# Third head's softmax before a slot's first piece, MLP layer norms on ScalarE within the fc products, weight sums in halves, the last product by token tiles

## Chip, cores and metric

One core of a Trainium2 chip. The metric is the device time of one execution in microseconds (us), the median of several runs. The engines run side by side and wait for one another by semaphores: PE (TensorE, matmuls and transposes), DVE (VectorE), ACT (ScalarE), POOL (GpSimd) and SP (SyncE, which here only issues DMA transfers). Each engine works off its own instructions in their given order, so an instruction that waits holds up all behind it on that engine.

## The reference

A block of cross attention with an MLP behind it, in float32, for 8 batches of 256 tokens, width D = 512, 16 heads of 32, inner width 2048:

```python
def layer_norm(x, w, b):
    mu = jnp.mean(x, axis=-1, keepdims=True)
    var = jnp.mean(jnp.square(x - mu), axis=-1, keepdims=True)
    return (x - mu) * jax.lax.rsqrt(var + EPS) * w + b
...
residual = hidden_states
x = layer_norm(hidden_states, ln1_w, ln1_b)
q = (x @ q_w + q_b)       # k and v the same from encoder_hidden_states; split into 16 heads
scores = jnp.einsum('bhqd,bhkd->bhqk', q, k) * scale
scores = jnp.where(mask, scores, mask_value)
attn = jax.nn.softmax(scores, axis=-1)
out = jnp.einsum('bhqk,bhkd->bhqd', attn, v)
out = out @ cproj_w + cproj_b
hidden = out + residual
residual = hidden
y = layer_norm(hidden, ln2_w, ln2_b)
y = jax.nn.gelu(y @ fc_w + fc_b, approximate=True)
y = y @ proj_w + proj_b
return residual + y
```

## The kernel before

**Tiling.** The tokens go in four groups g of 512 (two batches each). All large products (q, k, v, the output projection, fc and proj) are Strassen products in Winograd's form: the two operands are cut in quarters "11", "12", "21", "22", sums of quarters ("s1" to "s4" of one side, "t1" to "t4" of the other) are made by DVE or POOL, and PE does seven products of quarters in place of eight. A product's result is in a PSUM bank; DVE adds banks and stored sums (u1, u2, u3) into the four quarters of the result. u1 is a copy by ACT, u2 = bank 6 + u1, u3 = bank 7 + u2; the quarters of fc's result are called h, and x within group 0.

**Attention, 0 to 343 us.** Lines 866 to 897 write out the order by hand. There are 32 units, one for each group of four heads and batch. Unit n issues the scores of unit n+2 (PE, `s`, L572), then the softmax of unit n+2's four heads one by one between other work. `softmax(n, j)` is, twice, a masked row maximum on DVE (L590) and an exp on ACT (L600). `turn_probs(n, j)` transposes a head's probabilities (PE, `ppt`, L625), which DVE copies to `pt` for head 0 and ACT for heads 1 to 3 (L630). `divide(n+1)` is four multiplications on POOL (L614). `attend(n)` multiplies pt with v (PE, `av`, L641). Between these stand, in two slots of each unit (`between[g, u, 0]` and `[g, u, 1]`), pieces of other groups' Strassen products: a few matmuls (L367) and their evacuation on DVE or ACT (L386, L384). The unit's order before is: scores and softmax 0 of n+2; transposes 0 and 1; divide; softmax 1; the first slot's pieces; softmax 2; transposes 2 and 3; softmax 3; the second slot's pieces; attend. The transposes and av share two PSUM buffers.

**Output projection, 343 to 355 us.** Group 3's `po`.

**MLP, from 355 us.** For each group: fc with gelu, then proj with the residual added (`resm`, in the code `ht`), and the result stored.

- Group 0's fc (355.1 to 404.4 us) goes by quarter-columns q = 0 to 3. In each of them PE does the seven products in the order 11·11, s2·t2, s3·12, 21·t1, 12·21, 22·t4, s4·22. In the last two quarter-columns `splits` forms further sums of fc's weights (`split_sums`, four operations of 128x256 for each quarter n and half r), which the groups 1 to 3 use. They are formed in a `stage` of three buffers used in turn (`w_stage` in the trace), and two DMAs on SP store each set to `w2_dram` (L973, L974); a buffer is free when its stores have landed. The table `SPLITS` says which engine forms which set at which of the places 0 to 2 of a quarter-column.
- Groups 1 to 3's fc is seven `product(k)` calls with weights read back from `w2_dram`.
- The proj part is seven products `py` between which stands the next group's layer norm: statistics on DVE (L194, L195), roots on POOL (L199, L200) and the normalisation of four token tiles on DVE (`hm`, L203), all issued after the first and second product. `turn_next(c)` then transposes a column chunk of hm (PE, `pyt`, L216) and DVE scales it into y (L244). The loads of hm (`load_hid`, SP, L179) are issued by `load_next`: in group 0 after quarter-column 0, in the others after product 1.
- The last product of a group is 22·t4 on a bank that already holds a product; its sum is added to `ht` (L927) and two token tiles of 128x512 are stored (L1281).

`add` (L927) is a helper: operations of DVE and POOL in the MLP all carry its line, and are told apart by their tiles.

Of the kernel before, what the change touches and what calls it, by code (L numbers as in the profile page):

```python
# [16 lines left out]
P = 128  # L17
# [5 lines left out]
def tile_xattn_block(  # L23
# [100 lines left out]
    def col(base, i):  # L124
        return cols[:, base + i : base + i + 1]
# [60 lines left out]
    def layer_norm(tiles, tag, eng=nc.vector):  # L186


        mv = small.tile([P, NT, 2], F32, tag="mv", name=f"mv_{tag}")
        rstd = small.tile([P, NT], F32, tag="rstd", name=f"rstd_{tag}")  # L190

        def stats(t):
            st = small.tile([P, nc.vector.BN_STATS_DIM], F32, tag="st", name=f"st_{tag}_{t}")
            nc.vector.bn_stats(st, tiles[t])  # L194
            nc.vector.bn_aggr(mv[:, t, :], st)  # L195

        def roots():
            ve = small.tile([P, NT], F32, tag="ve", name=f"ve_{tag}")
            nc.gpsimd.tensor_scalar_add(ve, mv[:, :, 1], EPS)  # L199
            nc.gpsimd.tensor_tensor(rstd, ve, neg_half, ALU.pow)  # L200

        def normalise(t):
            eng.tensor_scalar(  # L203
                tiles[t], tiles[t], mv[:, t, 0:1], rstd[:, t : t + 1], ALU.subtract, ALU.mult
            )
# [34 lines left out]
    def turn_hid(ps, g, c):  # L240
        if c == 0:
            ys[g] = tokens_operand(both, "cT", f"y_{g}")
        turn(ps, hids[g], c)
        nc.vector.tensor_scalar(  # L244
            chunk(ys[g], c), halves(ps), col(c_ln2w, c), col(c_ln2b, c), ALU.mult, ALU.add
        )


    with ExitStack() as att:
# [557 lines left out]
        def run(pieces):  # L807
            for p in pieces:
                p()
# [57 lines left out]
        for n, (g, hg, b) in enumerate(units):  # L867
            u = hg * GB + b
            ahead = n + 2 < len(units)
            if ahead:  # L870
                scores(n + 2)
                softmax(n + 2, 0)
            run(aside[g, u, 0])
            turn_probs(n, 0)
            turn_probs(n, 1)
            if n + 1 < len(units):
                divide(n + 1)
            if ahead:
                softmax(n + 2, 1)
            run(between[g, u, 0])  # L880
            if ahead:
                softmax(n + 2, 2)
            turn_probs(n, 2)
            turn_probs(n, 3)
            run(aside[g, u, 1])
            if ahead:
                softmax(n + 2, 3)
            run(between[g, u, 1])
            run(aside[g, u, 2])
            attend(n)  # L890
            run(later)
            later.clear()
            run(aside[g, u, 3])
# [12 lines left out]
    with ExitStack() as mlp:  # L906
# [19 lines left out]
        def add(eng, to, a, b, op=ALU.add):  # L926
            eng.tensor_tensor(to, a, b, op)  # L927
# [33 lines left out]
        stages = [0]  # L961

        def split_sums(eng, n, r):
            a, b = fcw[r][n], fcw[r + NQF // 2][n]
            st = stage[:, stages[0] % 3]
            stages[0] += 1
            s1, s2, s3, s4 = (st[:, i, :] for i in range(4))
            add(eng, s3, a[:, 0, :], b[:, 0, :], ALU.subtract)
            add(eng, s2, b[:, 1, :], s3, ALU.subtract)
            add(eng, s1, s2, a[:, 0, :])  # L970
            add(eng, s4, a[:, 1, :], s2, ALU.subtract)
            to = w2_dram[QI[n]][:, :, r * S : (r + 1) * S]
            nc.sync.dma_start(to[:, 2, :], s1)  # L973
            nc.sync.dma_start(to[:, 4:7, :], st[:, 1:, :])  # L974

        def keep_quarters(q):

# [43 lines left out]
        for g in range(NG):  # L1021
# [29 lines left out]
            def load_next():  # L1051
                if g + 1 < NG:
                    load_hid(g + 1)

            def bias_ht():

                for b, bias in ((0, projb[:, :HD2]), (1, pbd)):
                    o = out_quarter(b, 0)
                    add(GP, o, o, by_tiles(bias))

            if g == 0:
                y = ys[g]

                def fc(bank, w, b, q, first, last):
# [8 lines left out]
                            )  # L1073

                SPLITS = {
                    (2, 0): ((GP, "11", 0), (V, "12", 0)),
                    (2, 1): ((GP, "s2", 0),),
                    (2, 2): ((V, "s3", 0), (GP, "21", 0)),
                    (3, 0): ((GP, "s4", 0), (V, "22", 0)),
                    (3, 1): ((GP, "11", 1),),  # L1080
                    (3, 2): ((V, "12", 1), (GP, "s2", 1)),
                }

                def splits(q, at):
# [3 lines left out]
                for q in range(NQF):  # L1088
# [4 lines left out]
                    def by_h(t):  # L1093
                        return t.rearrange("p i (d s) -> p d i s", d=2)
# [39 lines left out]
                    gelu("22", 1, x["22"])  # L1134
                    fc(bank[7], "22", "t4", q, False, True)
                    add(V, x["12"], by_h(bank[7]), by_h(u2))
                    some_fc_sums(4)
                    some_pw(2)
                    gelu("12", 1, x["12"])
                    fc(bank[5], "s4", "22", q, False, True)  # L1140
                    add(V, x["21"], by_h(bank[5]), by_h(u2))
                    gelu("21", 0, x["21"])
                    sum_h("s3", q)
                    sum_h("s2", q)
# [6 lines left out]
                        keep_quarters(0)  # L1151
                    if q == 3:
                        bias_ht()
            else:
                gelus, parts = [], [0]

                def some_gelus(n=3):
                    for f in gelus[:n]:
                        f()
                    del gelus[:n]  # L1160
# [17 lines left out]
                def product(k, *sums):  # L1178
# [24 lines left out]

                    def made(cd, n, x):
                        some_gelus()
                        if sums[0][1] is None:
                            add(V, block(sums[0][0], cd), bank[n], x)
                            return

                        r = h["s3"][:, parts[0] % 4 // 2, parts[0] % 2 * HF // 2 :][:, : HF // 2]  # L1210
                        parts[0] += 1
                        add(V, r, bank[n], x)
                        for to, base in sums:
                            add(GP, block(to, cd), block(base, cd), r)
# [29 lines left out]


                product(0, ("21", None))
                product(1, ("11", "21"))
                gelu("11", 0)
                ht = residual(work, hid_dram[g], "resm", f"resm_{g}")
                load_next()  # L1250
                product(2, ("21", "21"))
                product(3, ("12", "21"))
                product(4, ("22", "12"), ("21", "21"))
                product(5, ("21", "21"))
                gelu("21", 0)
                gelu("22", 1)
                product(6, ("12", "12"))
                some_gelus(len(gelus))
                gelu("12", 1)
                for which in ("s3", "s2"):  # L1260
# [3 lines left out]

            bank = {n: bank_of(n, f"py{n}") for n in (1, 7, 6, 5)}

            def proj(bank, a, w, first, last):
                for i in range(2):
# [9 lines left out]
            def store(b):  # L1278
                for i in range(2):
                    r = g * NT + 2 * b + i  # L1280
                    nc.sync.dma_start(of[ts(r, P), :], ht[:, 2 * b + i, :])  # L1281

            def turn_next(c):
                if g + 1 < NG:
# [14 lines left out]
                load_w2(1, 1)  # L1299
            else:  # L1300
                some_gelus(HF)
            if g + 1 < NG:
                seen, roots, normalise = layer_norm(hids[g + 1], f"m{g + 1}")
                for f in (*seen, roots):
                    f()
            for q in range(NQF):
                sum_h("s1", q)
            proj(bank[7], "s3", "12", True, False)
            if g + 1 < NG:
                for f in normalise:  # L1310
                    f()
            if g == 0:
                split_sums(GP, "s4", 1)
                split_sums(V, "22", 1)
# [78 lines left out]
```

## Time and profile before

| what | value |
|---|---|
| median of 3 runs | 745.24 us (745.17 to 746.19) |
| the profiled execution's time | 745.05 us |
| its span in the profile | 743.0 us |
| attention | 0 to 343.0 us |
| group 0: fc, then proj | 355.1 to 404.4, then to 456.4 us |
| groups 1 to 3 | 456.4 to 743.0 us |
| TensorE clock granted | 1.00 throughout |

Busy time by stage, in us, with the counts of instructions; the columns are the stretch, its length, then PE, PE's weight loads, DVE, ACT and POOL, and last the granted clock, the share of the DMA engines and GB/s:

```profile
0.00:343.00 343.00, 339.56 (x2542) 269.23 (x2543) 215.60 (x771) 226.95 (x706) 242.35 (x238) 1.00 0.45 144
343.00:355.10 12.10, 12.10 (x57) 10.65 (x58) 7.74 (x14) 0.47 (x1) 5.31 (x4) 1.00 0.39 116
355.10:404.40 49.30, 48.57 (x225) 42.46 (x224) 28.01 (x38) 15.47 (x33) 41.83 (x41) 1.00 0.86 287
404.40:456.40 52.00, 50.54 (x241) 44.23 (x240) 43.25 (x54) 1.81 (x4) 32.34 (x30) 1.00 0.68 238
456.40:743.00 286.60, 280.48 (x1881) 262.10 (x1879) 139.74 (x199) 53.02 (x120) 159.93 (x130) 1.00 0.38 141
```

PE is busy nearly everywhere, but matmuls are pipelined and their ends are modelled, so a group of matmuls with a wait inside shows as a longer group. The distance from one group's start to the next tells more than the busy share. Idle time of DVE, ACT or POOL costs nothing as long as what they make is there when PE asks for it. Where the profile gives a releaser for a wait, it is inferred.

### The profile page before, as it was taken

How to read it: one execution, taken by the hardware profiler on the slowest of the kernel's cores; microseconds unless marked ns; L12 is line 12 of the kernel's file. 1: busy time of each engine (PE TensorE's matmuls, PEld its weight loads, DVE VectorE, ACT ScalarE, POOL GpSimd, SP SyncE). 2: the span in 40 equal slices, each digit the busy share in tenths (PEclk: the TensorE clock that was granted, in tenths of full speed). 3: DMA queues.
4: the chain of work that ended last, by engine and by line, in shares of the span. 5: the costliest groups of instructions: out<-in, count | busy, mean ns of one | idle time of the engine just before them, and what ended most of it. 6: DMA issues, size and time to landing. Idle time of an engine off the chain costs nothing.

```text
span 743.0 us, 13604 instructions
## 1 busy us (share of the span) xinstructions
PE 731.2 (98%) x4941; PEld 628.7 (85%) x4941; DVE 434.3 (58%) x1075; ACT 297.7 (40%) x864; POOL 481.8 (65%) x441
## 2 busy tenths in 40 slices
PE   9999999999999999999999999999999999999997
PEld 8888777888787777678888789998899988999886
DVE  4676755676456566766267895663456634566111
ACT  2176777765777777761332000232002240031500
POOL 3856679667564469896877970579504796048960
PEclk9999999999999999999999999999999999999999
DMA  9614522552234166532796972992018930172001
GB/s 306 236 58 136 167 83 81 183 171 86 86 100 161 58 209 229 187 109 91 245 348 223 307 280 67 344 361 92 1 57 314 379 116 1 57 270 85 1 1 56
DMA packets 79426, 117.82 MB, mean 159 GB/s; under 512 B 6612, under 2 KB 57856, under 8 KB 77696
## 3 DMA queue, kind: packets, MB, share of 16 engines
q1 hardware_dynamic: 79104, 116.94, 46.0%
q8 instruction: 39, 0.64, 0.4%
q14 instruction: 27, 0.22, 0.1%
q0 software_dynamic: 256, 0.02, 0.0%
HBM read 85.48 MB, written 31.46 MB: 157 GB/s over the span
## 4 chain that ended last, share of the span: by engine, by line
PE 86%; DVE 5%; issue 3%; POOL 3%; ACT 2%; DVEq 0%; POOLq 0%
PE pf L924 23%; PE py L924 19%; PE ppt L625 7%; PE pqT L367 7%; PE pv L367 5%; PE po L367 5%; PE s L572 5%; PE av L641 5%; PE pkT L367 5%; DVE hm L203 2%; PE pkT L464 2%; ACT pr L600 2%; POOL h L927 1%; DVE w_stage L927 1%; PE pxt L216 1%
## 5 line engine op out<-in xcount | busy, mean ns | idle before, releaser
L614 POOL TENSOR_TENSOR pr<-pr,rsum 128x512 f32<-128x512 f32 x128 | 130.2, 1048 | 74.9 <-DVE rsum L612 43.7
L927 POOL TENSOR_TENSOR h<-h,hs 128x512 f32<-128x512 f32 x79 | 98.6, 1276 | 108.8 <-DVE hs L927 108.5
L600 ACT ACTIVATE pr<-pr,nmax 128x256 f32<-128x256 f32 x256 | 128.1, 503 | 61.3 <-DVE nmax L590 61.2
L924 PEld LDWEIGHTS pf<-y,w 128*128 128x128 f32 x1176 | 131.8, 192 | 0.2
L924 PE MATMUL pf<-y,w 128*128 128x128 f32 x1176 | 131.8, 275 | 0.0
L590 DVE CUSTOM_DVE_ANT_0 pr<-s,mb 128x256 f32<-128x256 f32 x256 | 94.0, 413 | 42.0 <-PE s L572 35.0
L1218 ACT COPY u<-pf 128x512 f32<-128x512 f32 x21 | 12.3, 585 | 216.0 <-PE pf L924 216.0
L924 PE MATMUL py<-pw,h 128*128 128x256 f32 x384 | 84.9, 379 | 0.0
L924 PE MATMUL py<-pw_t,h 128*128 128x256 f32 x384 | 84.2, 379 | 0.0
L924 PEld LDWEIGHTS py<-pw_t,h 128*128 128x128 f32 x384 | 72.7, 190 | 9.8
L924 PEld LDWEIGHTS py<-pw,h 128*128 128x128 f32 x384 | 72.5, 190 | 9.6
L625 PEld LDWEIGHTS ppt<-ident,pr 128*128 128x128 f32 x512 | 57.3, 141 | 14.8 <-issue 9.9
L625 PE MATMUL ppt<-ident,pr 128*128 128x128 f32 x512 | 68.7, 276 | 0.2
L927 DVE TENSOR_TENSOR u<-pf,u 128x512 f32<-128x512 f32 x50 | 34.5, 691 | 37.9 <-PE pf L924 33.7
L630 ACT COPY pt<-ppt 128x512 f32<-128x512 f32 x96 | 51.6, 570 | 4.9 <-PE ppt L625 4.9
L367 PE MATMUL pv<-vw,ctxT 128*128 128x256 f32 x224 | 52.4, 380 | 0.0
L367 PE MATMUL pqT<-xnT,qw 128*128 128x256 f32 x224 | 51.2, 380 | 0.3 <-issue 0.3
L924 PE MATMUL pf<-y,fcw 128*128 128x256 f32 x224 | 48.8, 379 | 0.7 <-DVE u L927 0.7
L600 ACT ACTIVATION_READ_ACCUMULATOR pr<-pr,nmax 128x1 f32 x256 | 48.5, 189 | 0.0
L924 PEld LDWEIGHTS pf<-y,fcw 128*128 128x128 f32 x224 | 42.5, 190 | 6.9 <-DVE u L927 1.1
L367 PEld LDWEIGHTS pqT<-xnT,qw 128*128 128x128 f32 x224 | 41.3, 190 | 5.6 <-POOL ctxT L171 0.7
L367 PEld LDWEIGHTS pv<-vw,ctxT 128*128 128x128 f32 x224 | 41.0, 190 | 5.4 <-ACT xnT L341 0.3
(139 smaller groups left out, 1128.0 us busy)
## 6 DMA issues: line engine op xcount, KB each, us to landing
w<-w_dram SPq DMA_DIRECT2D x12, 1792.0 KB, 7.5
w<-in_L_xattn_fc_w_dram SPq DMA_DIRECT2D x27, 256.0 KB, 5.8
w<-w_dram SPq DMA_DIRECT2D x9, 768.0 KB, 7.3
w_dram<-w_stage SPq DMA_DIRECT2D x14, 384.0 KB, 2.9
ctx<-in_ctx_dram SPq DMA_DIRECT2D x16, 256.0 KB, 4.7
x<-in_x_dram SPq DMA_DIRECT2D x16, 256.0 KB, 4.8
v_dram<-st_v SPq DMA_DIRECT2D x16, 256.0 KB, 2.2
v<-v_dram SPq DMA_DIRECT2D x16, 256.0 KB, 3.5
```

Source lines behind the costliest of these rows:

```text
L203: eng.tensor_scalar(tiles[t], tiles[t], mv[:, t, 0:1], rstd[:, t : t + 1], ALU.subtract, ALU.mult)
L367: nc.tensor.matmul(bank[n][:, i, :], l[:, c, ts(i, P)], r[:, c, :], start=first and i == 0 and c == 0, stop=last and c == HC - 1, skip_gro ...
L464: nc.tensor.matmul(bank[:, i, :], w[f"{n[0]}{j + 1}"][:, c, ts(i, P)], x()[f"{j + 1}{n[1]}"][:, c, :], start=at == 0, stop=j == 1 and c == ...
L572: nc.tensor.matmul(banks[j][:, i, :], qT[j * HD : (j + 1) * HD, b * S + i * P : b * S + (i + 1) * P], kT[j * HD : (j + 1) * HD, b * SK : ( ...
L590: nc.vector.tensor_tensor_reduce(pr[:, j, i, :], banks[j][:, i, :], mbias[g][1][:, b, :], scale=-SCALE, scalar=FLT_MAX, op0=ALU.add, op1=A ...
L600: nc.scalar.activation(pr[:, j, i, :], pr[:, j, i, :], AF.Exp, bias=nmax[:, j, i : i + 1], scale=-1.0, accum_out=sums[:, j, i : i + 1],)
L614: nc.gpsimd.tensor_tensor(pr[:, j], pr[:, j], rsum[:, j, :, None].to_broadcast([P, NQ, SK]), ALU.mult,)
L625: nc.tensor.transpose(ps[:, kc, ts(i, P)], probs[n][:, j, i, ts(kc, P)], ident)
L630: nc.scalar.copy(pt, ps)
L641: nc.tensor.matmul(av[j * HD : (j + 1) * HD, :], vs[g, hg][:, b * NK + kc, ts(j, HD)], pts[n, j][:, kc, :], start=(kc == 0), stop=(kc == N ...
L924: nc.tensor.matmul(ps, lhsT, rhs, start=first, stop=last, skip_group_check=True)
L927: eng.tensor_tensor(to, a, b, op)
```

## The change

Four parts.

1. **Attention.** The softmax of the third head (index 2) of unit n+2 is issued ahead of the first slot's pieces instead of behind them.
2. **Layer norm of the next group in the MLP.** `norm_piece` issues one of its small steps at a time: four statistics (DVE), the roots (POOL), and a new `shift` (DVE, −mean·rstd, 128x4). In group 0 they are issued in quarter-columns 1 to 3 after the add of x["12"] and after that of x["21"]; in groups 1 and 2 within products 3 and 4, and after products 5 and 6. The normalisation itself, `normalise_next`, is four ACT instructions (identity with scale rstd and bias shift) instead of four on DVE, issued at the end of group 0's fc, or after the first product of proj in the others. `turn_next` comes two products earlier, and the scaling into y is on ACT for groups 1 to 3. The loads of hm are issued one product earlier in groups 1 and 2.
3. **Group 0's weight sums.** `split_sums` can do its first two or its last two operations; VectorE's sets are issued in two halves at successive places (a new place 3 is behind the add of x["12"]). The two stores of a set are issued with the second half. POOL's sets stay whole.
4. **Last product of the last group.** The right half of the columns of the second pair of token tiles is stored ahead of the last product; the product is issued one token tile after the other, each with its own add of 128x256 and its own store of half a row block.

```diff
@@ attention, one unit
             if ahead:
                 softmax(n + 2, 1)
+                softmax(n + 2, 2)
             run(between[g, u, 0])
-            if ahead:
-                softmax(n + 2, 2)
             turn_probs(n, 2)
@@ turn_hid
-        nc.vector.tensor_scalar(
-            chunk(ys[g], c), halves(ps), col(c_ln2w, c), col(c_ln2b, c), ALU.mult, ALU.add
-        )
+        w, b = col(c_ln2w, c), col(c_ln2b, c)
+        if g == 0:
+            nc.vector.tensor_scalar(chunk(ys[g], c), halves(ps), w, b, ALU.mult, ALU.add)
+        else:
+            nc.scalar.activation(chunk(ys[g], c), halves(ps), AF.Identity, bias=b, scale=w)
@@ split_sums
-        def split_sums(eng, n, r):
+        def split_sums(eng, n, r, half=None):
             a, b = fcw[r][n], fcw[r + NQF // 2][n]
-            st = stage[:, stages[0] % 3]
-            stages[0] += 1
+            if half != 1:
+                staged_sums[n, r] = stage[:, stages[0] % 3]
+                stages[0] += 1
+            st = staged_sums[n, r]
             s1, s2, s3, s4 = (st[:, i, :] for i in range(4))
...
+            if half != 1:
+                add(eng, s3, a[:, 0, :], b[:, 0, :], ALU.subtract)
+                add(eng, s2, b[:, 1, :], s3, ALU.subtract)
+            if half != 0:
+                add(eng, s1, s2, a[:, 0, :])
+                add(eng, s4, a[:, 1, :], s2, ALU.subtract)
+                to = w2_dram[QI[n]][:, :, r * S : (r + 1) * S]
+                nc.sync.dma_start(to[:, 2, :], s1)
+                nc.sync.dma_start(to[:, 4:7, :], st[:, 1:, :])
@@ the layer norm in steps (new)
+            def norm_next():
+                seen, roots, _ = layer_norm(hids[g + 1], f"m{g + 1}")
+                mv, rstd = layer_norm.last
+                nm = small.tile([P, NT], F32, tag="nm", name=f"nm_{g + 1}")
+                def shift():
+                    nc.vector.scalar_tensor_tensor(nm, mv[:, :, 0], -1.0, rstd, ALU.mult, ALU.mult)
+                norm.extend([*seen, roots, shift])
+                return nm, rstd
...
+            def normalise_next():
+                if g + 1 < NG:
+                    nm, rstd = norm_of[0]
+                    for t, xt in enumerate(hids[g + 1]):
+                        nc.scalar.activation(
+                            xt, xt, AF.Identity, bias=nm[:, t : t + 1], scale=rstd[:, t : t + 1]
+                        )
@@ SPLITS
-                    (2, 0): ((GP, "11", 0), (V, "12", 0)),
-                    (2, 1): ((GP, "s2", 0),),
-                    (2, 2): ((V, "s3", 0), (GP, "21", 0)),
-                    (3, 0): ((GP, "s4", 0), (V, "22", 0)),
-                    (3, 1): ((GP, "11", 1),),
-                    (3, 2): ((V, "12", 1), (GP, "s2", 1)),
+                    (2, 0): ((GP, "11", 0), (V, "12", 0, 0)),
+                    (2, 1): ((GP, "s2", 0), (V, "12", 0, 1)),
+                    (2, 2): ((V, "s3", 0, 0), (GP, "21", 0)),
+                    (2, 3): ((V, "s3", 0, 1),),
+                    (3, 0): ((GP, "s4", 0), (V, "22", 0, 0)),
+                    (3, 1): ((GP, "11", 1), (V, "22", 0, 1)),
+                    (3, 2): ((V, "12", 1, 0), (GP, "s2", 1)),
+                    (3, 3): ((V, "12", 1, 1),),
@@ a quarter-column of group 0's fc
                     add(V, x["12"], by_h(bank[7]), by_h(u2))
+                    splits(q, 3)
+                    some_norm(q, 0, 1, 1, 0)
...
                     add(V, x["21"], by_h(bank[5]), by_h(u2))
+                    some_norm(q, 0, 1, 2, 1)
...
                     if q == 3:
                         bias_ht()
+                        normalise_next()
@@ product(k) of groups 1 to 3
                         some_gelus()
+                        if k in (3, 4) and cd != "22":
+                            norm_piece()
...
                 product(0, ("21", None))
+                load_next()
                 product(1, ("11", "21"))
...
-                load_next()
...
                 product(5, ("21", "21"))
+                norm_piece()
...
                 product(6, ("12", "12"))
+                norm_piece()
@@ proj
             else:
                 some_gelus(HF)
-            if g + 1 < NG:
-                seen, roots, normalise = layer_norm(hids[g + 1], f"m{g + 1}")
-                for f in (*seen, roots):
-                    f()
+                normalise_next()
...
             proj(bank[7], "s3", "12", True, False)
-            if g + 1 < NG:
-                for f in normalise:
-                    f()
+            turn_next(0)
+            turn_next(1)
...
-            turn_next(0)
-            turn_next(1)
+            turn_next(2)
+            turn_next(3)
...
-            turn_next(2)
-            turn_next(3)
@@ the last product
-            proj(bank[7], "22", "t4", False, True)
-            o_add(V, 1, 0, bank[7])
-            store(1)
+                proj(bank[7], "22", "t4", False, True)
+                o_add(V, 1, 0, bank[7])
+                store(1)
+            else:
+                store(1, slice(HD2, D))
+                for i in range(2):
+                    proj(bank[7], "22", "t4", False, True, (i,))
+                    o = ht[:, 2 + i, :HD2]
+                    add(V, o, bank[7][:, i, :], o)
+                    store(1, slice(HD2), (i,))
```

More of the change, by code (lines that the diff above doesn't have):

```diff
@@ L190, in layer_norm @@
         rstd = small.tile([P, NT], F32, tag="rstd", name=f"rstd_{tag}")
+        layer_norm.last = mv, rstd
         def stats(t):
@@ L960, in tile_xattn_block @@
         )
-        stages = [0]
-        def split_sums(eng, n, r):
+        stages, staged_sums = [0], {}
+        def split_sums(eng, n, r, half=None):
             a, b = fcw[r][n], fcw[r + NQF // 2][n]
-            st = stage[:, stages[0] % 3]
-            stages[0] += 1
+            if half != 1:
+                staged_sums[n, r] = stage[:, stages[0] % 3]
+                stages[0] += 1
+            st = staged_sums[n, r]
             s1, s2, s3, s4 = (st[:, i, :] for i in range(4))
[L968 to L974, printed above, removed]
+            if half != 1:
[7 more added lines that the diff above has]
+                nc.sync.dma_start(to[:, 4:7, :], st[:, 1:, :])
         def keep_quarters(q):
@@ L1053, in load_next, with norm_piece, some_norm @@
                     load_hid(g + 1)
+            norm = []
+            def norm_next():
[6 more added lines that the diff above has]
+                return nm, rstd
+            def norm_piece():
+                if g + 1 < NG:
+                    if not norm_of:
+                        norm_of.append(norm_next())
+                    norm.pop(0)()
+            norm_of = []
+            def some_norm(q, *ns):
+                for _ in range(ns[q]):
+                    norm_piece()
+            def normalise_next():
+                if g + 1 < NG:
+                    nm, rstd = norm_of[0]
[3 more added lines that the diff above has]
+                        )
             def bias_ht():
@@ L1257, in tile_xattn_block @@
                 product(6, ("12", "12"))
+                norm_piece()
                 some_gelus(len(gelus))
@@ L1265, in tile_xattn_block, with proj @@
             bank = {n: bank_of(n, f"py{n}") for n in (1, 7, 6, 5)}
-            def proj(bank, a, w, first, last):
-                for i in range(2):
+            def proj(bank, a, w, first, last, tiles=(0, 1)):
+                for i in tiles:
                     for p in range(HF):
@@ L1276, in proj, with store @@
                         )
-            def store(b):
-                for i in range(2):
+            def store(b, cols_=slice(D), tiles=(0, 1)):
+                for i in tiles:
                     r = g * NT + 2 * b + i
-                    nc.sync.dma_start(of[ts(r, P), :], ht[:, 2 * b + i, :])
+                    nc.sync.dma_start(of[ts(r, P), cols_], ht[:, 2 * b + i, cols_])
             def turn_next(c):
```

## The prediction

> **What bounds the kernel now.** I read the page's shares and chain first, then the waits, then the timelines of three places, since an average over 743 us of unlike stages prices nothing.
>
> ```profile
> PE 731.2 (98%) x4941; PEld 628.7 (85%) x4941; DVE 434.3 (58%) x1075; ACT 297.7 (40%) x864; POOL 481.8 (65%) x441
> PE 86%; DVE 5%; issue 3%; POOL 3%; ACT 2%; DVEq 0%; POOLq 0%
> PE pyt L216 <- DVE hm L203: 3.1, 4, 1.1
> DVE w_stage L927 <- DMA w_dram<-w_stage: 4.6, 2, 3.2
> POOL w_stage L927 <- DMA w_dram<-w_stage: 3.0, 2, 2.5
> ```
>
> TensorE is the bound, and the matmul count stays as it is; only gaps of PE can be won. Some hide in "busy" PE: a group with a stall inside is only longer. So in the attention stage I compared groups. The chain of waits has this at one unit (start, us, engine and group); the last line is an undisturbed unit:
>
> ```profile
> 287.79 0.37 ACT pr L600
> 288.30 0.59 ACT pr L600 x2
> 288.88 0.48 ACT pt L630
> 289.41 1.53 PE av L641 x16
> ...
> 89.97 1.00 PE av L641 x16
> ```
>
> The third head's row maxima stand on DVE behind the evacuation of the slot's piece, so the two exps start late, the copy of pt for the last head but one stands behind them on ACT, and av waits for it: 0.53 in the group and 0.17 before it. Nine units from 258.5 to 331 have it, with periods of 8.08 to 8.15 us against 7.42 undisturbed.
>
> The timelines of PE, DVE, POOL and SP for the rest (in brackets the idle time before, and who ended it):
>
> ```profile
> 400.87 3.72 PE L924 MATMUL pf<-y,fcw 128*128 128x256 f32 x16 [0.73 <-DVE u L927]
> 427.31 0.76 PE L216 MATMUL pyt<-ident,hm 128*128 128x128 f32 x5 [1.08 <-DVE hm L203]
> 522.22 0.77 PE L216 MATMUL pyt<-ident,hm 128*128 128x128 f32 x5 [0.82 <-DVE hm L203]
> ...
> 371.26 3.15 SPq L179 DMA_DIRECT2D hm<-hid_dram  x4
> ...
> 391.60 0.82 POOL L927 TENSOR_TENSOR w_stage<-fcw,fcw 128x256 f32<-128x256 f32 x1 [0.51 <-DMA w_dram<-w_stage]
> 396.55 0.52 DVE L927 TENSOR_TENSOR w_stage<-fcw,fcw 128x256 f32<-128x256 f32 x1
> 738.62 0.69 DVE L927 TENSOR_TENSOR resm<-py,resm 128x512 f32<-128x512 f32 x1 [5.69 <-PE py L924]
> ```
>
> And the DMA view of the first of those hm loads (KB, us from issue to landing):
>
> ```profile
> hm<-hid_dram SPq DMA_DIRECT2D x1, 256.0 KB, 9.9
> ```
>
> The reader is to see the PE stalls that stand where the change works, when hm lands, that the staging buffers wait for their stores already, and the tail of 0.69 on DVE and its stores behind the last matmul.
>
> **What the Trainium skill says.** "DMA: Bandwidth & Descriptors", Anatomy of one DMA: a DMA's semaphore wait is on the issuing sequencer before dispatch, and a small transfer costs mostly its write receipt, about 2 us. So a store that isn't ready holds all later stores on SP. The trace agrees on the size: stage stores land after 1.7/2.5/4.6 us (least, median, most). "SBUF — State Buffer", Terms: VectorE and GpSimd lock a shared port pair and the loser blocks; here DVE's hm normalise takes 1356 ns in the MLP, and that of x 734. ScalarE has its own port. "ScalarE: Activation LUTs", Table sets: identity-like functions lie in every set, so normalising on ACT needs no reload (before has two loads of 1283 ns). "PSUM — Partial Sum Buffer", PSUM bank collisions: engines must be kept apart by bank; no run here shows what that costs the split last product yet.
>
> **The change, part by part.**
>
> *Third softmax ahead of the piece.* In the unit above, DVE's two maxima (413 ns each) go ahead of the 0.69-us evacuation, so the exps start some 0.8 earlier, pt is copied by about 0.8 earlier, and av, late by 0.17+0.53, no longer waits. Nine units by 0.67: 6.1. The unit at 117.8 has 0.66 of av stall: as well. Two score groups (at 108.4, where 16 matmuls take 2.23 instead of about 1.2, and at 117.8, 1.1) wait for ACT's xnT evacuation, which stands behind exps with 1.0 of idle ahead of them: 2.0. Small units 0.3. Against it: the piece's evacuation comes 0.8 later on DVE, but its bank is needed two pieces on (over 2.6 us); POOL's divides, busy 68.0 of 76.3 us from 266.7 to 343, become the next late thing and take back some 0.45. Sum −8.6; bounds −4.3 (half, if ACT or POOL takes the bound) and −9.5 (all that PE loses there).
>
> *Layer norms, groups 1 and 2 feeding 2 and 3.* PE waited 0.98 at 522 and 0.98 at 616 (step sizes). Statistics (671+182 ns a tile, four tiles) go beside products 3 and 4 on DVE, roots (1036) to POOL in an idle stretch of 1.3; ACT's gelus end at 506.9, four ACT normalises of about 0.75 (nearest row: ACT xnT 128x512, 771 ns) end near 509.9, the turns need them at 514. The loads of hm pass one 1-MB weight load on SP, which has slack of many us. y's evacuation goes from DVE (800 ns) to ACT (771), idle there. The turns themselves are the same sixteen transposes a group, two products earlier. All covered: −1.96; if ACT weren't done in time, each late us would come back as the same pyt wait, so the bounds are −1.96 and 0.
>
> *Group 0: split halves with statistics and normalise.* Meant to take away 0.9 (at 400) and 1.65 (425 to 427). But order counts:
> 1. Statistic 0 is put on DVE in quarter-column 1 after the add of 12 (378.4), while hm's first tile lands at 371.26+9.9 = 381.1. DVE stands 2.75 us; the add of 21, the gelu and POOL's sum hs behind it (before at 381.27) come 3.7 later: POOL starts at 384.9.
> 2. POOL's splits 11 and s2 end at 391.0 and 394.8. The stores of 12 now come in its second half, so they stand on SP behind those of s2: issued 395.3 and 395.8, landed (about 3) at 398.9. GpSimd's 21 takes the same stage buffer and starts at 398.9 instead of 391.60, ends 402.5.
> 3. VectorE's first half of s3 waits for the landing of 11's stores (393.7, before 390.07). So the adds of 12 and 21 in quarter 2 end at 395.7 and 399.0, statistic 3 at 399.8; ACT's gelus and then its copy u1 of quarter 3 follow at 400.5, and PE, which needs u1's bank back for the product of quarter 12, loses 1.3. The same chain costs 0.36+0.5 in quarter 2, where the gelu that step 1 delays holds u1 back until 385.4.
> 4. The stores of s3 again stand behind those of 21: issued at 403.0 and 403.6, landed near 406.6. VectorE's first half of 22 needs that buffer: 406.7 instead of 396.55. Behind it on DVE is u3, done at 409.1, for which PE's product 22·t4 waits. It started at 400.87 before; less its own stall of 0.9 and plus the 2.2 of step 3 it could start at 402.2: 6.9 are lost. fc ends 0.9+1.3+6.9−0.9 = 8.2 later.
> 5. After that POOL's last hs costs PE 0.3 more, but the pyt stalls of 1.65 are gone, since ACT, which is busy for 1.81 us of 404 to 456, normalises in time: net 8.2+0.3−1.65 = +6.9. Bounds: −2.5 if no store is late, and +12.9 if the three serial landings take the longest 4.6 instead of 2.6. I take the middle, since the order of issues on SP is given and 2.6 is the median in this window.
>
> *Last product by token tiles.* Same matmuls. In the compiled order the second tile's matmuls wait for the first tile's add, since both lie in one PSUM bank: 0.7 of PE. The final add is half as wide (0.42 instead of 0.69) and one 128-KB store stands last instead of the second of two issues 0.38 apart; half of the columns are stored before. −0.7+0.4 = −0.3; bounds −1.0 (PE doesn't stall) and +0.3.
>
> Sum: −8.6−1.96+6.9−0.3 = −3.96. The profiled execution took 745.05 (span 743.0), so 741.1; the median of the runs is 745.24, 0.2 above, so **741.3**.
>
> **The rivals.**
> - *The ring doesn't bind*: hm lands earlier than DVE gets there, stores land in 2, and the halves bring −2.5. 745.24−8.6−1.96−0.3−2.5 = 731.9. For it: before, those waits were only 4.6 and 3.0 in sum. Against: step 4 follows from the order of issues on one queue, whatever the times. 0.20.
> - *The ring costs more than all gains* (slower): the three landings that now follow one upon another (12 to 21, s3 to 22, 22 to the second s2) take 4.6 each, as stores among other traffic did at 400 to 403 (median 4.5), and group 0 pays 12.9. 745.24−10.86+12.9 = 747.3. It decides from 10.9 on, where group 0's loss eats the other parts' gain; with the measured median of 2.5 it is not reached. 0.18.
> - *Attention gives half*, −4.3, since ScalarE and POOL take up the bound of the units: 745.24−4.3−1.96−0.3+6.9 = 745.6. For it: POOL's 68.0 of 76.3; against: ACT had 0.70 idle directly ahead of the exps. 0.12.
>
> **How the numbers follow.** Forecast 0.50, own range 739 to 744; rivals 0.20, 0.18, 0.12. A measurement here tells 0.2% (1.5 us) from no change. Faster: 0.47 of the forecast and the first rival, 0.67. Same: 0.03 of it and 0.11 of the third, 0.14. Slower: the second and 0.01, 0.19. The range goes from 731.0 to 746.5: it takes in most of the first rival and the third, and leaves out the second and the first one's tail.
>
> **What would show it.** Right: av groups of 1.00 and periods near 7.4 from 258 to 331; no wait of pyt for hm; a wait of DVE's statistics for hm's DMA near 380; waits of w_stage for its stores well over 4.6+3.0; a PE gap of several us at 22·t4 of the fourth quarter-column, and about 0.7 in the last product. Wrong: fc of group 0 ending near 404 (first rival) or beyond 417 (second), or av still at 1.5.

## The result, and the profile after

The changed kernel takes 742.10 us (median of 5 runs, 741.05 to 742.28), the kernel before 745.45 (745.17 to 746.19, 5 runs): a ratio of 0.995 with a 95% interval of 0.9936 to 0.9965. 741.3 had been forecast. The profiled execution took 741.43, with a span of 739.7 against 743.0.

The waits view of the changed kernel (in all, times, longest, in us) answers to the lines shown of before:

```profile
DVE w_stage L929 <- DMA w_dram<-w_stage: 16.2, 3, 7.8
POOL w_stage L929 <- DMA w_dram<-w_stage: 8.5, 2, 4.2
PE pf L926 <- DVE u L929: 6.6, 2, 6.1
```

The wait of pyt for hm is no longer in it, the waits for the stage buffers have gone from 4.6 and 3.0 to 16.2 and 8.5, and PE has a wait of 6.1 us for a u3. The longest of them on DVE, 7.8, falls in group 0's proj and costs PE nothing. Where the time went is read from the starts of PE's groups in both timelines, since the matmuls are the same:

| stage | before | after | difference | predicted |
|---|---|---|---|---|
| to the start of group 0's fc | 355.08 | 346.38 | −8.70 | −8.6 |
| group 0's fc | 49.34 | 58.83 | +9.49 | +8.2 |
| group 0's proj | 52.00 | 50.10 | −1.90 | −1.35 (0.3−1.65) |
| groups 1 and 2 | 189.81 | 187.74 | −2.07 | −1.96 |
| group 3 to the end of the span | 96.77 | 96.65 | −0.12 | −0.3 |
| sum | 743.0 | 739.7 | −3.30 | −3.96 (group 0 in sum taken as 6.9) |

The chain of waits of the changed kernel in the unit that corresponds to the one shown of before:

```profile
281.84 0.87 PE ppt L628 x8
282.71 1.73 PE po L370 x8
284.44 1.00 PE av L644 x16
285.44 0.62 PE s L575 x5
```

av follows the piece at once and takes 1.00 instead of 1.53; the chain no longer leaves PE here. All units from 255 to 315 have a period of 7.43 us. ACT shows why, in its timeline:

```profile
282.63 0.50 ACT L603 ACTIVATE pr<-pr,nmax 128x256 f32<-128x256 f32 x1
283.03 0.19 ACT L603 ACTIVATION_READ_ACCUMULATOR pr<-pr,nmax 128x1 f32 x1
283.12 1.05 ACT L633 COPY pt<-ppt 128x512 f32<-128x512 f32 x2
```

The third head's exps are over at 283.22, when the piece's matmuls still run, and both copies of pt at 284.17, ahead of av at 284.44.

Group 0's fc gives it back. The timelines of DVE and POOL, and of SP for the stores:

```profile
372.54 0.70 DVE L195 BATCH_NORM_STATS2 st_m<-hm 128x6 f32<-128x512 f32 x1 [2.79 <-DMA hm<-hid_dram]
...
376.25 1.27 POOL L929 TENSOR_TENSOR hs<-h,h 128x512 f32<-128x512 f32 x1 [7.65 <-ACT h L1141]
385.79 0.37 SPq L980 DMA_DIRECT2D w_dram<-w_stage  x1
386.26 0.44 SPq L979 DMA_DIRECT2D w_dram<-w_stage  x1
386.79 0.53 SPq L980 DMA_DIRECT2D w_dram<-w_stage  x1
390.00 0.73 POOL L929 TENSOR_TENSOR w_stage<-fcw,fcw 128x256 f32<-128x256 f32 x1 [4.24 <-DMA w_dram<-w_stage]
397.18 0.69 DVE L929 TENSOR_TENSOR w_stage<-fcw,fcw 128x256 f32<-128x256 f32 x1 [5.21 <-DMA w_dram<-w_stage]
```

Read from the top: DVE stands 2.79 us for hm, and POOL begins its sums late. VectorE had set 12 ready at 381.0, but its two stores are issued only at 386.26 and 386.79, behind the store of s2 at 385.79, which had to wait for POOL's last operation of s2. So POOL's set 21 waits 4.24 for the buffer that 12 holds, its stores go out late in turn, those of s3 behind them, and VectorE's first half of 22 stands 5.21. PE meets the end of it:

```profile
391.30 1.99 PE L926 MATMUL pf<-y,fcw 128*128 128x256 f32 x8 [0.35 <-ACT u L1162]
399.39 5.98 PE L926 MATMUL pf<-y,fcw 128*128 128x256 f32 x16 [6.10 <-DVE u L929]
```

Besides the stall, the sixteen matmuls behind it take 5.98 where the same sixteen took 3.72 before. The windows of the changed kernel (stretch, its length, busy PE, PE's weight loads, DVE, ACT, POOL, then the granted clock):

```profile
393.30:399.40 6.10, 0.01 (x1) 0.01 (x1) 2.18 (x4) 0.84 (x2) 5.86 (x7) 0.82 0.73 253
399.39:403.40 4.01, 4.01 (x10) 3.20 (x11) 2.86 (x5) 0.91 (x2) 3.85 (x5) 0.50 0.40 135
```

TensorE's clock is at 0.50 for more than four microseconds after the stall. That costs 2.4 us, which the prediction did not have.

### The profile page after: what moved, and what is told of

Its sections match the earlier page's. It is cut to its first block, busy times and chain, and to the rows that moved or that the text cites. A ratio compares the mean times of both kernels' runs of the same rounds, so it can differ in the third digit from the quotient of the medians.

```text
span 739.7 us, 13634 instructions
## 1 busy us (share of the span) xinstructions
PE 725.8 (98%) x4941; PEld 627.5 (85%) x4941; DVE 407.2 (55%) x1055; ACT 312.4 (42%) x888; POOL 478.8 (65%) x441
## 4 chain that ended last, share of the span: by engine, by line
PE 92%; DMA 3%; SPq 1%; POOL 1%; DVE 1%; issue 0%; ACT 0%; DVEq 0%; POOLq 0%
PE py L926 26%; PE pf L926 19%; PE ppt L628 8%; PE pv L370 7%; PE po L370 7%; PE pqT L370 7%; PE pkT L370 5%; PE s L575 5%; PE av L644 4%; PE pkT L467 2%; DMA hm<-hid_dram 1%; DMA w_dram<-w_stage 1%; PE pyt L217 1%; PE pxt L217 1%; POOL w_stage L929 1%; SPq L935 1%
## 5 line engine op out<-in xcount | busy, mean ns | idle before, releaser
L628 PEld LDWEIGHTS ppt<-ident,pr 128*128 128x128 f32 x512 | 57.5, 141 | 14.6 <-issue 9.3
L929 DVE TENSOR_TENSOR resm<-py,resm 128x512 f32<-128x512 f32 (+1 forms) x21 | 13.6, 663 | 85.5 <-PE py L926 85.5
L926 PE MATMUL pf<-y,fcw 128*128 128x256 f32 x224 | 52.0, 393 | 7.0 <-DVE u L929 6.6
```

Of the source, the lines that this page charges most:

```text
L628: nc.tensor.transpose(ps[:, kc, ts(i, P)], probs[n][:, j, i, ts(kc, P)], ident)
L926: nc.tensor.matmul(ps, lhsT, rhs, start=first, stop=last, skip_group_check=True)
```

## The experiments

The theory to be tested was that two things make group 0's loss: the wait for hm in quarter-column 1 and the order of the stores on SP. The first rival was that the wait alone does it, and that the order is harmless.

**Statistics out of quarter-column 1.** The changed kernel with

```diff
-                    some_norm(q, 0, 1, 1, 0)
+                    some_norm(q, 0, 0, 2, 0)
...
-                    some_norm(q, 0, 1, 2, 1)
+                    some_norm(q, 0, 0, 3, 1)
```

> The changed kernel with no statistic in group 0's quarter-column 1: two after each add of quarter-column 2, the roots after them, the shift in quarter-column 3. Theory 'order of stores': GpSimd starts its sums 3.7 us earlier, s2 is done near 382.1, the stores of 12 still stand behind those of s2 and land near 385.9, those of s3 behind those of 21 and land near 393.4, so VectorE still waits for a stage buffer (first half of 22) and PE still stalls before product 22·t4, but 2 to 3 us instead of 6.3, and the clock dips less or not: 735 to 737.5 us. Rival 'the wait for hm alone': without it every store is in time, the stall is gone, 732 to 733.5 us.

Measured: 737.31 us, 0.9889 of before (0.9875 to 0.9904), 4.8 below the changed kernel. Its timelines of POOL, DVE and PE:

```profile
371.80 1.26 POOL L929 TENSOR_TENSOR hs<-h,h 128x512 f32<-128x512 f32 x1 [3.97 <-ACT h L1141]
385.68 0.73 POOL L929 TENSOR_TENSOR w_stage<-fcw,fcw 128x256 f32<-128x256 f32 x1 [4.23 <-DMA w_dram<-w_stage]
393.19 0.42 DVE L929 TENSOR_TENSOR w_stage<-fcw,fcw 128x256 f32<-128x256 f32 x1 [4.67 <-DMA w_dram<-w_stage]
395.13 6.28 PE L926 MATMUL pf<-y,fcw 128*128 128x256 f32 x16 [4.46 <-DVE u L929]
```

The time is where the theory had it, near the upper end of the range. Counted from the start of fc, POOL begins 3.7 us earlier than in the changed kernel, yet its set 21 waits for 12's stores as long as before (4.23 and 4.24): that wait comes from the order of issues, not from the wait for hm. The stall was larger than the 2 to 3 us expected (4.46), as PE is earlier at this place too, and the slow clock came with it in full (6.28 in place of 3.72).

**Order of the stores.** The changed kernel with VectorE's second halves ahead of GpSimd's sets:

```diff
-                    (2, 1): ((GP, "s2", 0), (V, "12", 0, 1)),
-                    (2, 2): ((V, "s3", 0, 0), (GP, "21", 0)),
-                    (2, 3): ((V, "s3", 0, 1),),
+                    (2, 1): ((V, "12", 0, 1), (GP, "s2", 0)),
+                    (2, 2): ((V, "s3", 0, 0),),
+                    (2, 3): ((V, "s3", 0, 1), (GP, "21", 0)),
...
-                    (3, 1): ((GP, "11", 1), (V, "22", 0, 1)),
-                    (3, 2): ((V, "12", 1, 0), (GP, "s2", 1)),
-                    (3, 3): ((V, "12", 1, 1),),
+                    (3, 1): ((V, "22", 0, 1), (GP, "11", 1)),
+                    (3, 2): ((V, "12", 1, 0),),
+                    (3, 3): ((V, "12", 1, 1), (GP, "s2", 1)),
```

> The changed kernel with VectorE's second halves issued ahead of GpSimd's set of the same or an earlier place, so that their stores come first on SP; statistics as in the change, so VectorE still stands 2.8 us for hm. Theory 'order of stores': 21 and the first half of 22 find their stage buffers free, the stall of 6.3 and the slow clock of 2.6 behind it go, small stalls of 0.5 may stay: 732.5 to 734.5 us. Rival 'the wait for hm alone': the order does nothing, 741 to 742.5 us.

Measured: 737.64 us, 0.989 (0.9876 to 0.9905). The rival falls, as the order alone brings 4.5; but my number was 3 to 5 us too low. PE's timeline shows what I had taken for one small stall:

```profile
377.49 1.99 PE L926 MATMUL pf<-y,fcw 128*128 128x256 f32 x8 [0.21 <-ACT u L1162]
380.66 11.09 PE L926 MATMUL pf<-y,fcw 128*128 128x256 f32 x48 [1.18 <-DVE u L929]
393.59 1.99 PE L926 MATMUL pf<-y,fcw 128*128 128x256 f32 x8 [1.84 <-ACT u L1162]
396.65 1.99 PE L926 MATMUL pf<-y,fcw 128*128 128x256 f32 x8 [1.07 <-DVE u L929]
399.02 1.96 PE L926 MATMUL pf<-y,fcw 128*128 128x256 f32 x8 [0.38 <-DVE h L929]
```

PE idles 4.7 us in five pieces; each is short, and the clock stays full. Most of it is due to the wait for hm: in the kernel with both edits, which comes next, fc takes 49.77 us and here 54.78. Of these 5.0 us, 1.0 is paid again there, as PE waits 1.27 in its second proj product and 0.23 here.

**Both.**

> Both edits. Theory 'order of stores': group 0's fc takes 48.5 to 49 us with no PE stall, 0.5 to 1 us below the kernel with the order alone: 731.8 to 733 us. Rival 'the wait for hm alone': the same as with the statistics moved alone.

Measured: 734.19 us, 0.9847 (0.983 to 0.9863): 7.9 below the changed kernel, against 4.8 and 4.5 for one edit each. Each does something that the other doesn't, and they overlap by 1.4. It is 1 to 2 us above what I had expected. In its timelines PE still idles 1.09 before s4·22 and 1.27 in the second proj product, VectorE waits 4.77 for a stage buffer for the second half's set 12, and GpSimd 3.23 for the statistics ahead of the roots.

**Part 3 alone on the kernel before.**

> The kernel before with part 3 alone: VectorE's weight sums in halves, no statistics in fc, no other edit. Theory 'two causes': without the wait for hm GpSimd is on time, but the stores of 12 still stand behind those of s2 and the stores of s3 behind those of 21, so PE stalls some 4.5 us before product 22·t4 as in the kernel with the statistics moved, with 2.6 of slow clock behind it, less the 0.9 of the kernel before: 751 to 752.5 us. Rival 'halves hurt only together with the wait for hm': 744.5 to 745.5 us.

Measured: 751.55 us, 1.0069 (1.0046 to 1.0093), within the expected range. Here no statistic stands in fc; POOL's and PE's timelines:

```profile
396.41 0.73 POOL L927 TENSOR_TENSOR w_stage<-fcw,fcw 128x256 f32<-128x256 f32 x1 [4.24 <-DMA w_dram<-w_stage]
406.07 5.41 PE L924 MATMUL pf<-y,fcw 128*128 128x256 f32 x16 [4.86 <-DVE u L927]
```

The same wait of 4.24, the same stall of u3 and the slow clock behind it. So the halves with their late stores make the larger part of group 0's loss by themselves, 6.15 us by the medians (3.4 to 6.9 by the interval).

**Whole sums in the changed kernel,** with the table of the kernel before; first with the change's statistics, then with them moved as above.

> The changed kernel with VectorE's weight sums whole and at the places of the kernel before; statistics as in the change. Theory 'two causes': the stores come in the order in which they are ready, only the 2.8 us of the wait for hm and what GpSimd loses by it are left, with the whole set of 22 ahead of u3 (3.6 us on VectorE): 736.5 to 738.5 us, near the kernel with the order of stores mended. Rival 'the wait for hm outweighs the order': 740 us or more.

> As the one before with the statistics moved out of quarter-column 1 too. Theory 'two causes': no stall but that of u3 behind the whole set of 22 (0.9 to 1.7, as in the kernel with part 1 alone): 733.5 to 735.5 us. If the halves are worth more than the order costs them, it is above the kernel with both edits (734.2) by the 0.9 to 1.7.

Measured: 738.86 us, 0.9898 (0.9876 to 0.9921), and 735.28 us, 0.9857 (0.9831 to 0.9882). The first is at the upper edge, slightly above the range, the second within it. With the statistics moved, whole sums are 1.1 above halves in a good order, which is within the spread of the runs (734.0 to 737.24 and 733.31 to 734.82). The trace has a reason for it: PE waits 2.33 for u3 behind the whole set of 22. With the statistics as in the change, whole sums are 3.2 faster than the change, and the two intervals do not overlap.

**A version that removes what was left.** Both edits, and in addition the second half's sets 12 and s2 behind the last quarter-column's own sums, the roots ahead of them, and finally VectorE's halves of 22 behind u3:

```diff
-                    (3, 0): ((GP, "s4", 0), (V, "22", 0, 0)),
-                    (3, 1): ((V, "22", 0, 1), (GP, "11", 1)),
-                    (3, 2): ((V, "12", 1, 0),),
-                    (3, 3): ((V, "12", 1, 1), (GP, "s2", 1)),
+                    (3, 0): ((GP, "s4", 0),),
+                    (3, 1): ((V, "22", 0, 0),),
+                    (3, 2): ((V, "22", 0, 1), (GP, "11", 1)),
+                    (3, 4): ((V, "12", 1), (GP, "s2", 1)),
...
-                    some_norm(q, 0, 0, 3, 1)
+                    some_norm(q, 0, 0, 2, 1)
...
                     sum_h("s2", q)
+                    splits(q, 4)
```

The first place of `some_norm` has (0, 0, 2, 1) here as well. Without the move of 22:

> The kernel with both edits, but the sets 12 and s2 of the second half formed behind quarter-column 3's own sums, and the roots ahead of quarter-column 3's. It removes what was left there: VectorE's wait of 4.8 us for a stage buffer ahead of the add of 12, GpSimd's idle 3.2 us ahead of the roots, PE's 1.1 before s4·22 and 1.3 before the second proj product. Theory: 731 to 732.5 us. Rival: the later sets delay the loads of the next group's weights, which are then late at 448 us: 734 us or more.

and with it:

> The kernel with the second half's sets behind the quarter-column's own sums, and besides VectorE's halves of 22 one place later, behind u3, so that PE no longer waits 0.86 us for u3: 731.4 to 732.2 us, or no gain if the add of x22, which now stands behind a half, is late for s4·22: 732.3 to 733 us.

Measured: 732.59 us, 0.9817 (0.9797 to 0.9838), slightly above its range, with one wait of 0.86 for u3 left, and 731.18 us, 0.9806 (0.9793 to 0.9819), slightly better than expected. The PE timeline of the latter in group 0's fc is one line:

```profile
346.22 48.76 PE L926 MATMUL pf<-y,fcw 128*128 128x256 f32 x224
```

224 matmuls without a gap that the timeline lists. This version beats both kernels, by 14.6 us and by some 11.

**Part 1 alone on the kernel before.**

> The kernel before with part 1 alone. Theory: the attention stage's 9.0 us are its own, and all is kept to the end: 736 to 737 us, nine av groups of 1.00 us. Rival 'given back': the loads and stage stores behind it don't come earlier with it, and group 0 gives half back: 740 to 742 us.

Measured: 737.87 us, 0.9896 (0.9878 to 0.9915), above the expected range, with runs of 736.19, 736.94, 738.79 and 739.39. Group 0's fc starts at 346.46, so the attention stage gains 8.6 by itself, but not all of it is kept. The profiled run is the one of 739.39. Its PE timeline shows where 1.7 us went:

```profile
418.54 0.33 PE L216 MATMUL pyt<-ident,hm 128*128 128x128 f32 x1 [0.71 <-DVE hm L203]
419.94 0.77 PE L216 MATMUL pyt<-ident,hm 128*128 128x128 f32 x5 [1.07 <-DVE hm L203]
420.54 8.76 PE L923 MATMUL py<-pw_t,h 128*128 128x256 f32 x32
```

Behind two stalls for hm, 32 matmuls take 8.76 where they took 7.07 in the kernel before. Before u3 PE idles 1.65 there (0.73 before). The mean granted clock tells the four runs apart: it is 0.996 in the two longer ones and 1.000 in the two shorter ones, which lie within the expected range.

**The stall and the clock.** The kernel before, with u2's add done 2 or 5 times more in the last quarter-column, so that u3 is late by a chosen amount (the edit for 2):

```diff
                     fc(bank[7], "s3", "12", q, True, False)
+                    for _ in range(2 if q == 3 else 0):
+                        add(V, u2, bank[6], u1)
                     add(V, u3, bank[7], u2)
```

> The kernel before with the add that makes u2 done twice more in the last quarter-column of group 0's fc, so that u3 and PE's product 22·t4 come some 1.25 us later (0.62 each, as adds follow one another on VectorE). Theory 'a stall lowers TensorE's clock only when it is long': the stall grows from 0.73 to about 2.0, the sixteen matmuls behind it keep 3.7 us, 746.5 to 747 us. Rival 'any stall of 2 us may lower it': they take 5.4 us, 748 to 749 us.

> The same with five more adds: the stall grows by 3.1 to about 3.8 us. Theory: now the matmuls behind it run at half the clock for some four microseconds and take 6.0 to 6.3 instead of 3.7, as after the stalls of 4.5 and 6.1; 750.5 to 751.5 us, that is 2.3 to 2.6 more than the stall itself. Rival 'the slow matmuls come from what else ran at the time': 748 to 749 us.

Measured: 747.01 us, 1.0014 (1.0007 to 1.002), at the upper end of its range, and 749.48 us, 1.0049 (1.0035 to 1.0062). The two kernels' PE timelines, and the clock in the windows of the second (columns as above):

```profile
403.03 3.72 PE L924 MATMUL pf<-y,fcw 128*128 128x256 f32 x16 [2.62 <-DVE u L927]
```

```profile
404.53 5.97 PE L924 MATMUL pf<-y,fcw 128*128 128x256 f32 x16 [4.43 <-DVE u L927]
```

```profile
400.00:404.50 4.50, 0.10 (x1) 0.00 (x0) 4.24 (x7) 0.84 (x2) 4.27 (x6) 0.75 0.57 188
404.50:408.50 4.00, 3.97 (x9) 3.19 (x10) 3.78 (x6) 0.91 (x2) 2.63 (x4) 0.50 0.57 185
```

In these two profiled executions a stall of 2.62 leaves the matmuls behind it at 3.72, and one of 4.43 brings the half clock and 2.25 more. So a stall in the kernel before, with nothing of the change, is enough. The stall of 2.62 probably doesn't always go free: the profiled execution, 746.30 us, is one of four out of twenty with a mean granted clock of 0.999 or more (median 746.2); the sixteen others have a median of 747.1. The time of the second kernel is below the expected range because the pyt stall of 1.9 behind it nearly vanished: PE is 5.9 us later there, DVE's statistics only 4.2.

**Part 4 alone on the kernel before.**

> The kernel before with part 4 alone. As predicted: PE gains nothing and loses 0.6 to 0.7 between the two token tiles, the narrower add and the single last store give it back: 745.0 to 745.4 us, beside 745.4 to 745.6 of the kernel before. Rival 'the split pays': PE doesn't stall, 744.5 us or less.

Measured: 745.74 us beside 745.81, 0.9997 (0.9989 to 1.0004): no difference that can be told. PE's timeline, the last product's two token tiles:

```profile
724.36 10.52 PE L924 MATMUL py<-pw_t,h 128*128 128x256 f32 x48
735.47 3.72 PE L924 MATMUL py<-pw_t,h 128*128 128x256 f32 x16 [0.59 <-DVE resm L927]
```

The second tile's sixteen matmuls wait 0.59 for the first tile's add. This is what the prediction read in the compiled order; at the other end the narrower add takes 0.42, and the last transfer lands 1.7 us after its issue. The rival, a gain of about 1 us, lies outside the interval (a gain of at most 0.8).

Part 2 was not run alone: what it gains in groups 1 and 2 and in group 0's proj is read from the traces, in which the waits of pyt for hm are gone. A fourth stage buffer, which might take the waits for buffers away without touching the order, was not tried either.

## Why the prediction was right

The forecast of 741.3 holds against 742.1, and the likeliest case was the one that came. The terms have the right signs, and the mechanism was the one forecast. That the sum is so close is in part luck: within group 0 three misses, −1.1, +2.4 and −0.55 us, come to only +0.7.

- *Attention* (−8.6): −8.70, and −9.0 if the first scores' later start (0.3 us, ahead of the change's first effect) is taken out. The 0.45 that POOL was to take back did not show: the nine units are at 7.43, with 0.01 lost in each. The two score stalls of 2.0 were won but for 0.3 in one unit.
- *Group 0, step 1*: the wait for hm was put at 2.75 and is 2.79; step 2: POOL's 21 was to start at 398.9, which less the 8.7 that everything is earlier makes 390.2, and starts at 390.00; step 4: VectorE's first half of 22 at 406.7, less 8.7 makes 398.0, and it is 397.18. The stall was to be 6.9 and PE lost 6.26. Step 3's 0.86 and 1.3 are 0.66 and 1.16 (gaps between the starts of matmuls, over the 0.216 of an undisturbed step). So the chain was the one forecast and each link cost a little less than put down.
- *What was missing* in that sum is the clock behind the stall: from 399.39 to 405.21 sixteen matmuls take 5.82 instead of 16 times 0.216, so 2.37 more. Without it fc would have lost 7.1, 1.1 less than the 8.2 forecast. The prediction gave a stall no price beyond its own length.
- *Group 0's proj* won 1.90 rather than 1.35: the 0.3 of a late hs did not come, and the pyt stall before was 1.9 by the starts of the groups, not 1.65.
- *Groups 1 and 2*: −2.07 against −1.96. ACT's normalise takes 802 ns a tile, near the 0.75 assumed. It needed no table reload, as forecast: the trace has two loads of 1283 ns, as before.
- *Last product*: −0.12 in the trace against −0.3, both below what a measurement tells.

Of the rivals, the first (no store late) is refuted by the halves alone, which cost 6.15 in the kernel before; the second (landings of 4.6 each) by the stores concerned, those of 12, s3 and 22, whose two transfers landed after 2.5 and 3.1 each time; the third by the periods of 7.43. The 2 us that the prediction quotes from the Trainium skill, "DMA: Bandwidth & Descriptors", Anatomy of one DMA, are fitted there to DMAs issued by GpSimd; these stores go out on SP, and the sum used landing times of the trace. The prediction named the order of issues as what makes the buffers late "whatever the times", and two experiments bear that out: the wait for 21's buffer is 4.23 and 4.24 in kernels in which DVE does not wait for hm at all. Where my expectations failed afterwards, it was in taking one of the two causes for enough: mending the order still leaves most of 4.7 us of idle PE to the wait for hm.

## What to carry to other kernels

When work is split so that its last part comes later, its stores move too, and on a queue that issues in order they may end behind stores of another engine that are not ready yet; write down which buffer each of those stores frees before splitting. A small instruction put into an engine's order ahead of data that has not landed costs its wait to everything behind it, so place it by the landing time in the trace, not by where the engine seems free. And a gain elsewhere can hide such a loss: a change that is 3.4 us faster in sum held 11 more.

## What the runs showed of the hardware

The clock of TensorE after a stall is a price of its own: at 0.50, with matmuls starting every 0.427 us instead of 0.216. It cost 2.2 to 2.6 us behind stalls of 4.43, 4.46 and 6.10 us, but 1.7 behind one of 4.86 (the halves alone), 3.08 (whole sums as in the change) and 2.33 (whole sums with the statistics moved), and behind two of 0.71 and 1.07, 0.7 us apart (part 1 alone). A stall of 2.81, also in the kernel with whole sums as in the change, cost nothing. So the length alone does not decide.

The Trainium skill, "TensorE: Matmul & The Clock Gate", What's actually happening, says that the clock falls to half after at least one idle window of about 3.4 us, and that these windows run freely, without regard to the kernel. The traces agree with the windows: counted from where the clock changes, each trace falls into stretches of 3.41 us, and behind a stall the clock is at 0.50 for one whole stretch or for two. Here are the stretches around the stall of 2.33, around that of 2.81, and around that of 4.86, each with the one that follows (columns as above):

```profile
389.80:393.21 3.41, 1.08 (x5) 0.60 (x5) 3.36 (x3) 0.84 (x2) 3.26 (x3) 1.00 0.12 41
393.21:396.63 3.42, 3.42 (x8) 2.79 (x9) 1.29 (x2) 0.91 (x2) 3.26 (x5) 0.50 0.13 42
```

```profile
377.08:380.50 3.42, 1.74 (x9) 1.18 (x7) 3.35 (x5) 0.84 (x2) 3.26 (x4) 1.00 0.16 58
380.50:383.91 3.41, 2.29 (x11) 2.03 (x12) 2.87 (x4) 0.91 (x2) 3.25 (x5) 1.00 0.33 112
383.91:387.33 3.42, 3.42 (x17) 3.02 (x16) 2.23 (x4) 0.00 (x0) 2.40 (x4) 1.00 0.92 319
```

```profile
399.65:403.07 3.42, 1.56 (x8) 1.03 (x6) 0.00 (x0) 0.84 (x2) 3.26 (x4) 1.00 0.91 303
403.07:406.48 3.41, 0.41 (x2) 0.39 (x3) 2.87 (x5) 0.00 (x0) 3.25 (x5) 1.00 0.67 233
406.48:409.89 3.41, 3.41 (x10) 2.70 (x9) 3.31 (x6) 0.91 (x2) 2.44 (x3) 0.50 0.36 117
```

The stall of 2.33 lies within one stretch and leaves PE 1.08 us of work in it, and the next stretch is at half clock. The stall of 2.81 is shared by two stretches, with 1.74 and 2.29 us of work, and the clock stays. The stall of 4.86 begins in a stretch with 1.56 us of work, which passes; only the next stretch, with 0.41, brings half clock.

With the page's idle window the measurement does not agree: the stretch need not be idle throughout. In the fourteen traces, leaving out the first and last 10 us, the clock fell after stretches with 0.00 to 1.63 us of busy PE, and after none with more; the least that left it full was 1.56. So the border lies near 1.6 us, as the busy time counts it.

The prices follow from the stretches. One at half clock costs half of 3.41, 1.7 us. After the stalls of 4.43, 4.46 and 6.10 there were two, the first begun while PE still waited: in the changed kernel the half clock ends at 404.00, 4.6 us after the matmuls resume at 399.39, which makes 2.3, and 2.37 was measured. As the stretches don't start with the kernel, the same stall should cost in one execution and not in the next. That fits the twenty runs with the stall of 2.62 and the four with part 1 alone, but a trace of one execution of each is all there is, so for the others it is not shown.
